# Mask pieces written during group 0's own ranked units, exponents and squares shifted to ScalarE, and small loads moved, in a four-layer graph network

## The chip, the cores and the metric

The kernel runs on one core of a Trainium2 chip. The metric is the device time of one execution in microseconds (us). The engines are TensorE (PE in the profile), VectorE (DVE), ScalarE (ACT), GpSimd (POOL) and SyncE (SP), the last of which issues most transfers. Each engine takes its instructions in the order in which the program issued them.

## The reference

A graph of 3327 nodes with 64 features passes through four layers, each of which is `x = x + f(relu(layernorm(x)), adj)` with the same dense 3327 x 3327 matrix `adj` (few entries are not zero):

```python
# layer 0: two gated cells, h -> relu(ggc(h))
m = adj @ (x @ W); gi = m @ wih.T + bih; gh = x @ whh.T + bhh   # r, z, n gates, as in a GRU
# layer 1: only the pattern of adj and each entry's rank in its row count
mask = (adj != 0); rank = cumsum(mask, axis=1); deg = rank[:, -1:]
k = minimum(deg, 100.0); pos = rank - (deg - k)
w = mask * where(pos > 0, 0.5 ** (k - pos), 0.0)
out = w @ (input @ weight) + bias
# layer 2: w = adj * adj; three times x = (w @ x) @ W.T + b
# layer 3: twice x = tanh(concat([adj @ x, x]) @ W[k])
```

So there are eight products with an N x N matrix, called hops: hops 0 and 1 use `adj` (PLAIN), hop 2 the ranked weights (RANKED), hops 3 to 5 the squares (SQUARED), hops 6 and 7 `adj` again.

## The kernel before, in words

**Tiles and units.** The nodes are padded to 2 x 13 blocks of 128. The 13 block columns are cut into four chunks (3, 3, 3 and 4 blocks, thus 384 or 512 columns for each of two halves), and the chunks into two groups, chunks 0 and 1 in group 0 and chunks 2 and 3 in group 1. A `Tile` is one of 26 source blocks of `adj`'s transpose for one group, 768 or 896 KB; 20 buffers (`slots`) hold tiles and, in halves of a buffer, masks. A unit is (hop, chunk, tile): it multiplies the tile's columns with the features of the source block into the chunk's PSUM sum (`propagate`, L561).

**Order.** `alone` and `joint` write a list of 914 units by hand. A tile serves two successive hops of its group before it is dropped, so group 0 and group 1 alternate: after group 0's hops 1 and 2, group 1 does hops 2 and 3. A unit is *own* where its source block lies in the group that it computes. The last 26 units of group 0's hop 2 (288 to 313 in the list) are own ones, two of them special; units 314 on are those of group 1's hop 2, two per tile, and its first hop-3 unit is 326.

**Looking ahead.** `run` goes through the list. In step i it issues loads up to 44 units ahead while buffers are free, makes masks up to 24 units ahead (`make_mask`, which takes room for a mask and queues two pieces), prepares squares 6 units ahead (`prepare`, L404) and expands ranked weights 3 units ahead (`expand`), and then propagates unit i.

**A ranked unit.** A mask piece is one VectorE instruction of 127 x 896 (or 768) elements (L427), and the last row comes by a small transfer from GpSimd's queue (L432). `expand` multiplies the mask by the triangular matrix `tri` on TensorE (`mm`, L271), for the two halves s = 0 and 1, and turns each half into the bits of a power of two, on ScalarE (L477) or on VectorE (L475). A tile's pieces are written by `mask_pieces(1)` once per step, except in group 0's own units, or are forced by `expand` (L468) where they are not there yet. The special unit adds the last rows of all blocks from a list, `lastw`, made by `last_sources` (L512 to L531).

**Ends of hops.** When a chunk's sum is complete, a generator (`after_0` to `after_7`) is begun. What it does is cut by `yield us`, and it continues when the scheduler's count of TensorE time (`spend`) has gone that far, or at once where something needs its result (`finish`). `after_1` ends with the layer norm and the three-term split of y[2] and, later, with `add_row(c, 3)` (L795), which adds layer 1's bias to x. `after_2` evacuates the sum (L702 or L704), does the dense product with `bd`, adds to x (L789), and makes y[3] by `layernorm_relu` (L767 to L782): sums, mean, difference, squares (on VectorE at L774 or on ScalarE at L772), their sum, a power on GpSimd (L778), and the product. The special unit of a chunk finishes the generators of the other chunks.

**Constants.** `more_constants` is such a generator, too: it loads the weights of the second cell (`load_cell(1)`), the dense weights `bd`, the last layer's `w3` (w in the profile), and the bias rows `brow`.

Of the kernel before, what the change touches and what calls it, by code (L numbers as in the profile page):

```python
# [52 lines left out]
NC = 4  # L53
PARTS = (4, 5)
CWM = 512
GROUPS = [(0, 1), (2, 3)]
# [35 lines left out]
def upper(n):  # L92
    return slice(n * D, (n + 1) * D)
# [3 lines left out]
def kernel(  # L97
# [58 lines left out]
    def unfold_cell(cell):  # L156

        n = 3 * D + (NBIAS if cell == 0 else 0)
        i, ps = take()
        for h in range(2):  # L160
            nc.tensor.matmul(ps[upper(h), :n], ident[:, :D], stage[:, 4 * D:4 * D + n], start=True, stop=True)
        v = ps[:, :3 * D].rearrange("p (g f) -> p g f", f=D)
        for h in range(2):
            nc.vector.tensor_copy(cells[upper(1 - h), cell, h, 0:3], v[upper(1 - h)])
        if cell == 0:
            nc.vector.tensor_copy(bcol, ps[:, 3 * D:n])
        give(i)
# [36 lines left out]
    def more_constants():  # L204
        nc.gpsimd.memset(stage, 0.0)
        nc.gpsimd.memset(cells, 0.0)
        for c in range(NC):
            for h in range(2):
                nc.gpsimd.memset(both[c][upper(h), h], 0.0)
        nc.gpsimd.memset(bd, 0.0)  # L210
        yield 5.0
        load_cell(0)
        yield 20.0
        unfold_cell(0)
        yield 1.0

        full = work.tile([P, P], BF16, name="t2")
        nc.gpsimd.memset(full, -TWO7)
        nc.gpsimd.affine_select(out=tri, in_=full, pattern=[[-1, P]], compare_op=ALU.is_gt, fill=0.0,
                                base=0, channel_multiplier=1)  # L220
        nc.gpsimd.affine_select(out=tri, in_=tri, pattern=[[-1, P]], compare_op=ALU.not_equal, fill=TWO7 * TWO7,
                                base=0, channel_multiplier=1)
        nc.gpsimd.memset(tri[:, P - 1:P], 0.0)
        nc.gpsimd.memset(bitsb, BITS)
        nc.gpsimd.memset(lasty, 0.0)
        wide = work.tile([P, P], F32, name="t2")
        nc.gpsimd.memset(wide, 0.0)

        for i, (bi, bh) in enumerate(((BI1, BH1), (BI2, BH2))):
            nc.vector.tensor_add(bsum[:, i], bcol[:, bi:bi + 2], bcol[:, bh:bh + 2])  # L230

        nc.vector.tensor_scalar(wide[0:D], wide[0:D], bcol[0:D, BL1:BL1 + 1], None, op0=ALU.add)
        yield 3.0
        i, ps = take()
        mm(ps[:, :D], wide, ident[:, :D])
        nc.vector.tensor_copy(brow[:, 3], ps[:, :D])
        give(i)
        yield 1.0
        yield from fold_cell(0)
        for c in range(NC):  # L240
            yield 1.0
            ahead_of_cell(c)
        yield 50.0
        load_cell(1)
        yield 10.0
        for h in range(2):
            nc.sync.dma_start(out=bd[upper(h), :, upper(h)], in_=weights[:, WL1:WL3])
            for i in range(2):
                nc.sync.dma_start(out=w3[upper(h), :, i], in_=weights[:, WL3 + (h + i) % 2:NW:2])
        yield 10.0  # L250
        unfold_cell(1)
        yield from fold_cell(1)
        yield 20.0
        nc.sync.dma_start(
            out=brow[:, 0:3],
            in_=bass.AP(tensor=bias_rows.tensor, offset=bias_rows.offset, ap=[[0, P], [D, 3], [1, D]]),
        )
# [35 lines left out]
    def give(i):  # L293
        released[i] = max(released) + 1
        (idle_sums if i < 4 else idle_temps).append(i)
# [29 lines left out]
    def begin(c, task):  # L325
        finish(c)
        tasks[c] = [task, 0.0]
        advance(c)
# [5 lines left out]
    def later_task(us, task):  # L334
        yield us
        yield from task
# [10 lines left out]
    y = [[None] * NC for _ in range(8)]  # L347
# [90 lines left out]
    def mask_pieces(n=0, t=None):  # L438

        while pieces and (n > 0 or any(u is t for u, _, _ in pieces)):  # L440
            _, half, piece = pieces.popleft()
            piece(half)
            n -= 1

    def expand(k, c, t):

        if k == COUNT:
            return None
        w = width(c)
        if t is SPECIAL:  # L450
            g = c // 2
            w0 = (CH[c][0] - CH[GROUPS[g][0]][0]) * P
            finish(NC + 1 + g)
            return lastw[g][:, w0:w0 + w].bitcast(BF16)
        if KIND[k] == PLAIN or (KIND[k] == SQUARED and t.in_place):
            return t.view(c)
        if KIND[k] == SQUARED:
            room = Mask(t.w)
            wide = room.view.rearrange("p s w -> p (s w)").bitcast(F32)[:, :2 * w].rearrange("p (s w) -> p s w", s=2)
            square(wide, t.view(c), t.q + c)  # L460
            squared[k, c, t] = room
            return wide
        wide = work.tile([P, 2, CWM], I16, name="e", bufs=4)[:, :, :w]

        mask_pieces(t=t)  # L468
        for s in range(2):
            i, ps = take()  # L470
            mm(ps[:, :w], tri, t.mask.view[:, s, t.cols(c)])
            own = chunk_of(t.q % NB) in GROUPS[t.g]
            busy = any((k - 1, ch) in sums for ch in GROUPS[t.g])
            if s and (own if t.g == 0 and (own or busy) else c == GROUPS[t.g][1] or t.g == 1 and not own):
                nc.vector.tensor_scalar(wide[:, s], ps[:, :w], BITS, 0.0, op0=ALU.add, op1=ALU.max)  # L475
            else:
                nc.scalar.activation(wide[:, s], ps[:, :w], AF.Relu, bias=bitsb)  # L477
            give(i)
        spend(STREAM_US * w / CWM * 0.5)
        if c == GROUPS[t.g][1]:  # L480
            t.mask.free()
        return wide.bitcast(BF16)
# [182 lines left out]
    def run():  # L665
        total = {}
        for k, c, t in units:
            total[k, c] = total.get((k, c), 0) + 1
        done = {}
        loaded, masked, prepared, expanded = 0, 0, 0, deque()  # L670
        for i, (k, c, t) in enumerate(units):
            while loaded < len(units) and loaded < i + LOAD:
                u = units[loaded][2]
                if u is not SPECIAL and u.slot is None:
                    if len(dead) <= RESERVE and loaded > i + EXPAND:
                        break
                    u.load()
                loaded += 1
            while masked < min(loaded, i + MASK):
                if is_masked(*units[masked]):  # L680
                    if not spare and len(dead) <= RESERVE + 1:
                        break
                    make_mask(units[masked][2], RANKED)
                masked += 1
            while prepared < min(loaded, i + PREPARE):
                prepare(*units[prepared])
                prepared += 1
            while len(expanded) < min(EXPAND + 1, len(units) - i):
                assert prepared > i + len(expanded)
                expanded.append(expand(*units[i + len(expanded)]))  # L690
            if k != 2:
                mask_pieces(1 + len(pieces) // 6)
            elif not (c in GROUPS[0] and (t is SPECIAL or chunk_of(t.q % NB) in GROUPS[0])):
                mask_pieces(1)
            n = done[k, c] = done.get((k, c), 0) + 1
            propagate(k, c, t, expanded.popleft(), n == 1, n == total[k, c])

# [183 lines left out]
    def after_1(c, acc):  # L881
        pace = 1.0 if c in GROUPS[0] else 1.2
        at, h2T = yield from gru(acc, c, BI2, BH2, 1, pace)
        v = transpose_to_nodes(h2T, c)
        dead.append(at)
        yield 0.8 * pace
        residual(v, c, relu=True)
        yk = nodes(c)
        yield from layernorm_relu(yk, c, TWO27, 1.2 * pace, squares_on_scalar=c in GROUPS[1])
        y[2][c] = yield from in_three(yk, c)  # L890
        yield 45.0 if c in GROUPS[1] else 25.0
        add_row(c, 3)

    def after_2(c, acc):
        m = evacuate(acc, c)
        yield 1.4
        v = dense_to_nodes(m, WL1, c)
        yield 1.2
        residual(v, c)
        yk = nodes(c)  # L900
        yield from layernorm_relu(yk, c, pace=1.0)
        y[3][c] = yk
        yield 15.0
        add_row(c, 2)
# [67 lines left out]
            begin(c, before_0(c))  # L972
    begin(NC, more_constants())
    begin(NC + 1, later_task(70.0, last_sources(0)))
    begin(NC + 2, later_task(175.0, last_sources(1)))
    run()
    for c in list(tasks):
        finish(c)
# [39 lines left out]
```

## Time and profile before

| | us |
|---|---|
| median of 3 runs | 721.21 |
| lowest, highest of them | 721.14, 725.19 |
| profiled execution | 720.42 |
| its span, first to last instruction | 718.2 |
| TensorE busy in the span | 685.5 (95%) |
| VectorE busy | 343.5 (48%) |
| ScalarE busy | 264.4 (37%) |
| GpSimd busy | 79.2 (11%) |

A line of the profile names an engine, a source line, an operation, the tile written and the tile read, the size, and the number of instructions. In a timeline the first two numbers are start and duration in us, and a bracket at the end tells how long the engine had been idle and what ended it. In the page's slices each digit is a fortieth of the span.

### The profile page before, as it was taken

The page shows a single profiled execution, that of the slowest core. Times are in us where ns is not written, and L with a number is a line of the kernel's source. Part 1 is how long each engine was busy: PE and PEld are TensorE (multiplying, and loading weights), DVE is VectorE, ACT ScalarE, POOL GpSimd, SP SyncE. Part 2 cuts the span into 40 slices and gives each one's busy share as a digit, 9 for nine tenths or more (in the row PEclk, how much of TensorE's full clock was granted, in tenths as well). Part 3 has the DMA queues.
Part 4 walks back from the last instruction along what each step waited for, and adds up shares of the span by engine and source line. Part 5 has one row for each costly group of instructions (what it writes and reads, how often), then busy time and mean ns, then how long its engine had stood idle before and what let it go on. Part 6 is the DMA issues. An engine that isn't in the chain of part 4 may idle for free.

```text
span 718.2 us, 12625 instructions
## 1 busy us (share of the span) xinstructions
PE 685.5 (95%) x5128; PEld 354.0 (49%) x5128; DVE 343.5 (48%) x700; ACT 264.4 (37%) x403; POOL 79.2 (11%) x114
## 2 busy tenths in 40 slices
PE   1999999999999986999999999999999999999997
PEld 1454667544556763546444444334444444344464
DVE  7467736635987878847615102421162466005101
ACT  1014000302147853789999322850065700000101
POOL 4300000001491303212100000000010000000000
PEclk9999999999999998999999999999999999999999
DMA  9999994299678651492799839971997399927991
GB/s 346 401 386 405 406 395 160 61 374 377 228 272 315 232 191 52 144 320 92 243 359 373 285 109 406 405 295 57 375 372 260 116 391 405 405 97 262 400 402 39
DMA packets 68549, 201.31 MB, mean 280 GB/s; under 512 B 7228, under 2 KB 8228, under 8 KB 68492
## 3 DMA queue, kind: packets, MB, share of 16 engines
q1 hardware_dynamic: 65596, 199.46, 74.9%
q8 instruction: 40, 0.66, 0.4%
q10 hardware_dynamic: 720, 0.85, 0.3%
q0 software_dynamic: 2176, 0.20, 0.2%
q14 instruction: 17, 0.14, 0.1%
HBM read 199.45 MB, written 0.85 MB: 279 GB/s over the span
## 4 chain that ended last, share of the span: by engine, by line
PE 54%; ACT 4%; issue 1%; DVE 0%; ACTq 0%
PE sum L561 50%; ACT adj L404 4%; PE temp L271 3%; PE temp L723 1%; DVE both L758 0%; ACT both L757 0%; ACT t L702 0%; DVE xs L951 0%; PE sum L271 0%; ACTq L953 0%; ACT t L948 0%; ACTq L404 0%; ACT e L477 0%; ACTq L757 0%; ACTq L948 0%
## 5 line engine op out<-in xcount | busy, mean ns | idle before, releaser
L561 PE MATMUL sum<-adj,y 128*64 128x384 f32 (+3 forms) x3016 | 531.1, 501 | 2.1 <-DVE e L475 0.9
L561 PEld LDWEIGHTS sum<-adj,y 128*64 128x64 f32 x3016 | 228.6, 137 | 248.9 <-issue 222.7
L404 ACT ACTIVATE adj<-adj 128x768 f32<-128x768 f32 (+1 forms) x174 | 142.6, 890 | 49.5 <-PE sum L561 23.7
L427 DVE TENSOR_SCALAR adj<-adj 128x768 bf16<-128x768 f32 (+3 forms) x208 | 113.1, 594 | 37.8 <-PE temp L496 33.9
L477 ACT ACTIVATE e<-temp,bitsb 128x384 int16<-128x384 f32 (+1 forms) x114 | 64.7, 607 | 28.7 <-PE temp L271 19.7
L561 PE MATMUL sum<-e,both 128*64 128x384 bf16 (+1 forms) x624 | 74.6, 347 | 0.0
L758 DVE COPY both<-sum 64x384 f32<-64x384 f32 (+3 forms) x17 | 9.7, 568 | 115.6 <-ACT both L757 114.5
L757 ACT COPY both<-sum 64x384 f32<-64x384 f32 (+3 forms) x17 | 8.1, 478 | 153.0 <-PE sum L561 147.4
L406 DVE TENSOR_TENSOR adj<-adj 128x768 f32<-128x768 f32 (+1 forms) x34 | 32.6, 1010 | 53.5 <-DMA adj<-in_adjT 33.6
L778 POOL TENSOR_TENSOR st<-st,mhalf 128x6 f32<-128x6 f32 (+1 forms) x16 | 23.8, 1486 | 303.9 <-DVE st L776 303.9
L271 PE MATMUL temp<-adj,tri 128*64 128x384 bf16 (+1 forms) x334 | 51.7, 347 | 5.9 <-DVE adj L427 5.7
L561 PEld LDWEIGHTS <-both 128*64 128x64 bf16 x624 | 40.8, 112 | 19.3 <-issue 6.6
L432 POOL DMA_DIRECT2D adj<-totals x52 | 31.4, 605 | 119.9 <-DVE adj L836 74.8
L475 DVE TENSOR_SCALAR e<-temp 128x384 int16<-128x384 f32 (+1 forms) x53 | 32.2, 609 | 22.4 <-PE temp L271 10.7
L271 PEld LDWEIGHTS <-tri 128*64 128x64 bf16 x416 | 28.5, 112 | 27.7 <-issue 16.0
L752 DVE STREAM_TRANSPOSE both<-y 32x96 f32<-32x96 f32 (+1 forms) x128 | 35.6, 278 | 2.9
L704 DVE COPY t<-sum 128x384 f32<-128x384 f32 x8 | 4.4, 556 | 60.9 <-PE sum L561 60.9
L496 PE MATMUL temp<-adj,behind 128*64 128x384 bf16 x208 | 30.2, 339 | 0.9 <-DVE adj L427 0.7
L496 PEld LDWEIGHTS <-behind 128*64 128x64 bf16 x208 | 16.8, 110 | 17.7 <-issue 16.5
L702 ACT COPY t<-sum 128x384 f32<-128x384 f32 (+1 forms) x8 | 4.2, 529 | 54.2 <-PE sum L561 54.2
L914 DVE TENSOR_TENSOR y<-temp,brow 128x384 f32<-128x384 f32 (+1 forms) x8 | 4.7, 592 | 29.6 <-PE temp L271 29.6
L271 PE MATMUL sum<-adj,tri 128*64 128x384 bf16 (+1 forms) x82 | 15.5, 342 | 3.2 <-DVE adj L427 3.1
(121 smaller groups left out, 321.2 us busy)
## 6 DMA issues: line engine op xcount, KB each, us to landing
adj<-in_adjT SPq DMA_DIRECT2D x130, 768.0 KB, 8.8
adj<-in_adjT SPq DMA_DIRECT2D x104, 896.0 KB, 11.9
xs<-in_x SPq DMA_DIRECT2D x1, 640.0 KB
adj<-totals POOLq DMA_DIRECT2D x26, 3.0 KB, 4.8
adj<-totals POOLq DMA_DIRECT2D x26, 3.5 KB, 2.0
out<-xs ACTq DMA_DIRECT2D x2, 192.0 KB
out<-xs ACTq DMA_DIRECT2D x1, 256.0 KB
stage<-in_weights SPq DMA_DIRECT2D x2, 112.0 KB, 14.2
```

The source lines that it names most:

```text
L271: nc.tensor.matmul(out[hs], lhsT[:, hs], rhs, start=start, stop=stop)
L404: nc.scalar.activation(sq, v, AF.Square)
L406: nc.vector.tensor_tensor(sq, v, v, ALU.mult)
L427: nc.vector.tensor_scalar(t.mask.view[:rows, half], t.view()[:rows, half], 0.0, None, op0=ALU.not_equal)
L432: nc.gpsimd.dma_start(out=t.mask.view[P - 1:P], in_=totals[t.g][t.q:t.q + D + 1:D, :])
L475: nc.vector.tensor_scalar(wide[:, s], ps[:, :w], BITS, 0.0, op0=ALU.add, op1=ALU.max)
L477: nc.scalar.activation(wide[:, s], ps[:, :w], AF.Relu, bias=bitsb)
L496: nc.tensor.matmul(counts[c][1][s * D:(s + 1) * D, :w], behind[:, NQ - 1 - t.q:NQ - 1 - t.q + D], t.mask.view[:, s, t.cols(c)], start=firs ...
L561: nc.tensor.matmul(acc[h][1][h * D:(h + 1) * D, :w], yq[h], rhs[h], start=first and n == 0, stop=last and n == len(terms) - 1)
L752: nc.vector.transpose(to[at:at + 32, :, q], h[q * 32:(q + 1) * 32, :, s, f * 32:(f + 1) * 32])
L758: nc.vector.tensor_copy(both[c][upper(1), 1], acc[1][1][upper(1), :width(c)])
L778: nc.gpsimd.tensor_tensor(st[:, 3, :n], st[:, 2, :n], mhalf[:, :n], ALU.pow)
```

## The change

- In `run`, group 0's own units of hop 2 now call `mask_pieces(1)` too, in each third step, once y[2] of chunks 0 and 1 is there.
- In `expand`, while y[3] of chunk 0 or 1 is not there, a unit of group 1 with a source of group 0 gives the half s = 1 to VectorE only for chunk 3; chunk 2 gives both to ScalarE. Before, both chunks gave it to VectorE.
- In `after_2`, the squares of the layer norm of chunks 0 and 1 are taken by ScalarE.
- In `after_1`, the bias of layer 1 is added after 14 us of the scheduler's count for chunks 0 and 1 (25 before) and after 80 for chunks 2 and 3 (45 before).
- In `more_constants`, the second cell's weights are unfolded before `bd` and `w3` are loaded; those loads and that of `brow` come later by 41 and 15 us of the scheduler's count.
- `last_sources(1)` begins at 140 us of that count instead of 175.

```diff
@@ more_constants
         load_cell(1)
-        yield 10.0
+        yield 20.0
+        unfold_cell(1)
+        yield from fold_cell(1)
+        yield 30.0
         for h in range(2):
             nc.sync.dma_start(out=bd[upper(h), :, upper(h)], in_=weights[:, WL1:WL3])
             for i in range(2):
                 nc.sync.dma_start(out=w3[upper(h), :, i], in_=weights[:, WL3 + (h + i) % 2:NW:2])
-        yield 10.0
-        unfold_cell(1)
-        yield from fold_cell(1)
-        yield 20.0
+        yield 5.0
         nc.sync.dma_start(
             out=brow[:, 0:3],
...
@@ expand
             busy = any((k - 1, ch) in sums for ch in GROUPS[t.g])
-            if s and (own if t.g == 0 and (own or busy) else c == GROUPS[t.g][1] or t.g == 1 and not own):
+            if t.g == 1 and not own and any(y[3][ch] is None for ch in GROUPS[0]):
+
+                on_vector = s and c == GROUPS[1][1]
+            else:
+                on_vector = s and (own if t.g == 0 and (own or busy) else c == GROUPS[t.g][1] or t.g == 1 and not own)
+            if on_vector:
                 nc.vector.tensor_scalar(wide[:, s], ps[:, :w], BITS, 0.0, op0=ALU.add, op1=ALU.max)
             else:
                 nc.scalar.activation(wide[:, s], ps[:, :w], AF.Relu, bias=bitsb)
@@ run
             elif not (c in GROUPS[0] and (t is SPECIAL or chunk_of(t.q % NB) in GROUPS[0])):
                 mask_pieces(1)
+            elif i % 3 == 0 and all(y[2][ch] is not None for ch in GROUPS[0]):
+                mask_pieces(1)
@@ after_1
-        yield 45.0 if c in GROUPS[1] else 25.0
+        yield 80.0 if c in GROUPS[1] else 14.0
         add_row(c, 3)
@@ after_2
-        yield from layernorm_relu(yk, c, pace=1.0)
+        yield from layernorm_relu(yk, c, squares_on_scalar=c in GROUPS[0])
@@ tile_adj_gnn_stack_kernel
-    begin(NC + 2, later_task(175.0, last_sources(1)))
+    begin(NC + 2, later_task(140.0, last_sources(1)))
```

## The prediction, made before the changed kernel was run

> **What bounds the kernel now.** I read the page's slices first, then what TensorE waited for, then the busy table for the one stage that stands out, then that stage instruction by instruction.
>
> ```profile
> span 718.2 us, 12625 instructions
> PE   1999999999999986999999999999999999999997
> PEclk9999999999999998999999999999999999999999
> ```
> TensorE is the bound almost everywhere; its idle time is 718.2 - 685.5 = 32.7 us. Of it 15.0 is the start and some 4 the last 10 us. The only hole in between is in slices 15 and 16 (about 263 to 293 us), where the granted clock drops too.
>
> ```profile
> PE temp L740 <- DVE y L782: 15.0, 1, 15.0
> PE temp L271 <- DVE adj L427: 5.7, 6, 1.7
> PE sum L271 <- DVE adj L427: 3.1, 3, 2.1
> PE sum L561 <- DVE e L475: 0.9, 1, 0.9
> PE sum L561 <- DMA adj<-in_adjT: 0.7, 1, 0.7
> ```
> TensorE's waits: us in total, times, longest. After the start, what it waits for is VectorE: the ranked product by `tri` (L271) waits for the mask pieces of L427 (5.7 + 3.1 us).
>
> ```profile
> core 0: us, PE busy (x) PEld busy (x) DVE busy (x) ACT busy (x) POOL busy (x), PEclk, DMA share, GB/s
> 246.60:264.10 17.50, 17.41 (x218) 14.76 (x213) 14.46 (x28) 11.95 (x21) 1.01 (x2) 1.00 0.60 194
> 264.10:293.60 29.50, 19.82 (x166) 11.32 (x163) 24.48 (x49) 12.96 (x20) 10.03 (x13) 0.88 0.22 76
> 293.60:340.00 46.40, 46.40 (x414) 25.28 (x416) 30.86 (x55) 39.86 (x65) 7.03 (x13) 1.00 0.63 215
> 340.00:376.00 36.00, 35.17 (x264) 16.51 (x262) 14.55 (x27) 34.61 (x45) 2.98 (x2) 1.00 0.83 288
> ```
> The row 264 to 294: TensorE 19.82 of 29.5, VectorE 24.48, ScalarE only 12.96, transfers 0.22. VectorE paces this stage. In the row before (group 0's own ranked units) VectorE still has 3.0 us free, and no mask piece is written there.
>
> ```profile
> 263.77 0.54 DVE L789 TENSOR_TENSOR xs<-xs,temp 128x384 f32<-128x384 f32 x1
> 264.35 0.55 DVE L767 TENSOR_REDUCE st<-xs 128x6 f32<-128x384 f32 x1
> 264.94 0.17 DVE L768 TENSOR_SCALAR st<-st 128x6 f32<-128x6 f32 x1
> 265.15 0.56 DVE L769 TENSOR_TENSOR t<-xs,st 128x384 f32<-128x384 f32 x1
> 265.62 1.16 DVE L427 TENSOR_SCALAR adj<-adj 127x896 bf16<-127x896 f32 x2
> ...
> 269.67 0.55 DVE L774 TENSOR_TENSOR y<-t 128x384 f32<-128x384 f32 x1
> 270.26 0.55 DVE L775 TENSOR_REDUCE st<-y 128x6 f32<-128x384 f32 x1
> 270.84 0.17 DVE L776 TENSOR_SCALAR st<-st 128x6 f32<-128x6 f32 x1
> 270.92 1.16 DVE L427 TENSOR_SCALAR adj<-adj 127x896 bf16<-127x896 f32 x2
> ```
> VectorE in time order. The masks of group 1's first tiles are forced by `expand` (L468), three units before use, and stand in VectorE's queue behind the layer norm of group 0's chunk 0. TensorE idles 2.12 us to 266.29 and 1.68 us to 271.60 on these two pairs.
>
> **The Trainium skill.** "TensorE: Matmul & The Clock Gate", Part 1, says that the array falls to half clock after about a window of 3.4 us with little activity and returns after a busy one; the trace agrees (0.85 and 0.83 in 260-270 and 280-290, each behind over 2 us of idling, 1.00 elsewhere). "Perfetto Trace Analysis", Identifying the Most-Contended Engine, calls matmul busy time a bad measure; so here: the stage's busy 19.8 us covers only 14.3 us of work (below). "VectorE: DVE Perf Modes", Why PSUM operands drop a tier, explains why a piece of 896 elements from SBUF costs little more than an exponent instruction of 384 from PSUM; the trace: 0.54-0.62 us and 0.47-0.55.
>
> **Prices**, start to start in the trace. TensorE: `tri` products 0.33 (384 wide) and 0.43 (512), ranked sums 0.49 and 0.65, dense 0.66. VectorE: exponents (L475) 0.47 and 0.60, mask piece 0.54, L789, L767, L774, L775 0.58 each, L769, L782, L795, L704 0.47 each, L768 and L776 0.2. ScalarE: exponents 0.47 and 0.60, a square of 384 0.52 (L772). GpSimd's power 1.35 to 1.6.
>
> **What the stage could be.** From the first tri product of group 1 (266.29) to the start of the first squared unit (291.89) TensorE has 7 x (0.33 + 0.43) = 5.3 of tri products, 3 x 0.49 + 6 x (0.49 + 0.65) = 8.3 of sums and 0.66 dense: 14.3 us. Counted from 264.17, where TensorE ran dry, it took 27.7. So 13.4 us is the most that can be won before 292, and another 0.9 at 293.59.
>
> **The change, part by part.**
>
> *Mask pieces in own units.* The 26 own units last from about 246.6 to 272 now. Pieces can be queued from the fourth on (the horizon is 24 units); one in three units writes one: 8 pieces, the first four tiles. Both chunks' y[2] is complete when they begin (last L854 at 243.67). The tiles were issued for loading from 209 to 218, so no load is waited for. Cost: 0.54 per three units, 0.18 a unit; with the exponents 0.65 of TensorE's 0.81 per unit. It fits: 4.3 us for all eight against the 3.0 us that VectorE had free in that row and the 1.5 us of the list of last rows (L524 and L528, 0.5 + 1.0 at 250-252), which moves 35 us earlier by the scheduler's count, to about 216, where VectorE's row of mask pieces has just ended and TensorE is busy with plain units; ScalarE's 1.0 us (L530) goes with it. If this cover were missing, each piece would cost TensorE its 0.54. On GpSimd the pieces' row copies (L432, 0.54 each) now go out ahead of norm 0's power instead of behind it. What remains open is a wait for the mask's room, last read by recent tri products: 0 to 0.8 us a piece; I take 0, as the exponents before it wait for later tri products.
>
> *Exponents to ScalarE.* While group 0's y[3] is missing, the chunk-2 half goes to ScalarE: 0.47 less for each of the six or seven tiles to 291, with ScalarE 44% busy there. VectorE per tile: 2 x 0.54 + 0.60 = 1.7 instead of 2.15, TensorE 1.9.
>
> *Squares to ScalarE.* L774 goes from both norms: 2 x 0.58 less, with one wait of VectorE for ScalarE each, 0 to 1 us; I take 0 to 0.3. *Bias rows* (L795): chunks 0 and 1 go to about 256, and chunks 2 and 3 are forced at the special unit of chunk 0 instead: 0.47 + 0.60 there against 2 x 0.47 now. Nothing won.
>
> *Small weights.* Six DMAs (`bd`, `w3`; about 0.62 us of SP each, 3.7 in all, at 124-128) and `brow` (170) move to roughly 175-185 on SP, between loads that wait for room anyway; `bd` is read first at 262. Cover: the loads stand 44 units ahead. At best the 0.65 us wait for a load at 129.35 goes; 0 to 0.65 either way, I take 0.4 won.
>
> **The new stage, worked along the queues.** With the masks there, tri products never wait; the sums wait for exponents behind the norms.
> - Special unit of chunk 0 (260): a piece, two bias rows and L704 end at 262.45, 0.65 later than now, so TensorE is at the first group-1 tri product at 264.65.
> - Norm 0: L789 to L769 end at 266.7; an exponent 0.6, a piece, L775, L776 to 268.6. The special unit of chunk 1 then finishes this norm at once: L782 waits for GpSimd's power, to 270.3, with VectorE idle 1.7; L782 and L795 to 271.3, the next exponent to 271.9. TensorE waits 1.0.
> - Norm 1: 1.9 us of VectorE at 274-276, ahead of exponents: TensorE waits 1.5, then (L775, L776, two pieces) 0.9, then 0.7.
> Sum: 264.65 + 14.3 + 4.1 = 283.1 for the first squared unit, against 291.89: 8.8 us. The next unit starts at 283.75 against 293.59, since VectorE has made up its arrears: 9.8. No idle stretch reaches 2 us, so the half clock should go (its price is inside the 13.4). With the load wait 10.2.
>
> Profiled execution: 720.42 (span 718.2 and 2.2 around it) - 10.2 = 710.2; the median of the runs shown is 0.8 above it, so **711.0**.
>
> **Rivals.**
> - *VectorE still paces* (0.18). Its work did not shrink much: two norms (2 x 3.4 us) and two power waits (2 x 1.6) come to 10 us, and each can stall TensorE almost in full because exponents stand behind them in one queue. For: VectorE's 24.5 of 29.5. Against: three units of lookahead (2.5 us). Then some 9 of the 13.4 us stay: gain 4.5, 716.5.
> - *ScalarE gives it back* (0.07). It takes 7 x 0.47 + 2 x 0.52 = 4.3 us more, and is 34.6 of 36 us busy at 340-376, where the chain of waits runs through L404. If it reached that stage late, the 4.3 us would be paid there: 715.3. Against: it gains 0.45 us a tile on TensorE after 294.
> - *Slower* (0.04): each of the 8 pieces in own units holds VectorE until the room's last reader is done; VectorE cannot run ahead, and each costs the round trip of a tri product and exponent (0.33 + 0.56 + 0.25) with its own 0.54: 1.7 each, 13.5 in all, against 10.2 won: 724.5. It decides from 10.2/8 = 1.3 us a piece on.
>
> **Numbers.** The forecast's case (706 to 713.9) has 0.71: its stalls of 4.1 us could be 0.5 or 7. A measurement tells about 1% (7.2 us) from no change. Faster by over 1% (below 714.0) 0.71; within 1% 0.25 (the first two rivals); slower by over 1% 0.04. Range 706 to 717: most of the stalls gone, to VectorE still pacing.
>
> **What would show it.** Right: eight L427 pieces between 246 and 264, no wait of L271 for L427, clock 1.00 throughout, six or seven chunk-2 exponents on ScalarE, squares L772 twice more, VectorE idle 1 to 2 us ahead of L782 near 270, TensorE waits for L475 of 3 to 5 us in all, and the first squared unit near 283. Wrong: TensorE gaps between 248 and 262 (the slower case), over 7 us of waits for L475 (first rival), or a distance to before that shrinks after 340 (second).

## The result and the profile after

The changed kernel takes 712.87 us (median of 4 runs, 711.7 to 713.05) against 721.57 of the kernel before: 8.7 us less. The ratio is 0.9869, with a 95% interval from 0.9839 to 0.9899. The forecast was 711.0 us in a range from 706 to 717. The profiled execution took 712.98 us, with a span of 710.9.

The page's head and slices:

```profile
span 710.9 us, 12617 instructions
PE   1999999999999998999999999999999999999997
PEclk9999999999999999999999999999999999999999
```

The hole of slices 15 and 16 is down to a single 8, and the drops of the granted clock are gone. What TensorE waited for (us in total, times, longest), without the 14.9 us at the start:

```profile
PE sum L271 <- DVE e L480: 2.1, 2, 1.1
PE sum L566 <- DVE e L480: 1.8, 2, 1.6
PE sum L566 <- DMA adj<-in_adjT: 0.9, 2, 0.7
```

(Lines move by 5 to 7 in the changed file: the exponents on VectorE are L480 for L475, the sums L566 for L561, the power L785, and the product behind it L789.) No tri product waits for a mask any more. What is left in the stage are waits for exponents and one of 0.76 us for the evacuation of chunk 0's sum. The table by stage, engines from left to right as before:

```profile
246.60:264.10 17.50, 16.82 (x208) 14.27 (x203) 15.63 (x32) 11.89 (x21) 4.03 (x7) 1.00 0.41 124
264.10:284.00 19.90, 17.31 (x188) 12.82 (x190) 17.57 (x36) 14.47 (x27) 7.71 (x10) 1.00 0.38 127
```

The second row ends before the second hop-3 unit (286.29), where TensorE waits once more. Counted between the same units, from 4.5 us after the special unit of chunk 0 to the second hop-3 unit, the stage that took 29.5 us takes 20.7. VectorE is still the busiest engine in the row, 17.57 of 19.9 us against TensorE's 17.31.

**Where the 8.7 us are.** I cut each trace at three points: the special unit of chunk 0, the first hop-3 unit, and the ranked unit that follows the second hop-3 unit. From here on "the stage" is the time from the first of these points to the third.

| trace | special unit | first hop-3 unit | ranked unit after two | special to ranked | ranked to end |
|---|---|---|---|---|---|
| before | 259.61 | 291.89 | 294.50 | 34.89 | 423.75 |
| changed | 261.11 | 283.83 | 287.20 | 26.09 | 423.75 |

The stage gives 8.80 us, and what follows it takes the same 423.75 us in both. The spans differ by 7.3 only, because the changed kernel's profiled execution comes to the stage 1.5 us later. Most of that, 1.1 us, is at the start, where the program is the same; the first 48 sums:

```profile
16.34 8.70 PE L561 MATMUL sum<-adj,y 128*64 128x384 f32 x48
```

```profile
16.26 9.82 PE L566 MATMUL sum<-adj,y 128*64 128x384 f32 x48
```

The first line is of the kernel before, the second of the changed one. Over the traces of this study, from the first sum to the first counting product (L496, or L501 in the changed file), which follows these sums, it is 8.4 to 9.9 us, whatever the kernel: the records have TensorE at full clock from 17.9 us in the kernel before and from 20.1 in the changed one. A single profile is thus uncertain by about 1 us before the stage begins, and the experiments below are read by their stage as well as by their time.

**The share of the clock.** Up to the first hop-3 unit the stage is 9.6 us shorter. TensorE's busy time for the same products fell there from 23.4 to 19.4 us, and its idle time from 8.9 to 3.3 (the rows stand under "More pieces" below). The kernel before has two stretches of 3.4 us at half clock (granted clock 0.5) in it, the changed kernel none. So some 4 of the 9.6 us are busy time, most of it the clock, and 5.6 are waits that are gone.

### The profile page after: what moved, and what is told of

Same layout as the page of the kernel before. It is cut to its first block, busy times and chain, and to the rows that moved or that the text cites. A ratio compares the mean times of both kernels' runs of the same rounds, so it can differ in the third digit from the quotient of the medians.

```text
span 710.9 us, 12617 instructions
## 1 busy us (share of the span) xinstructions
PE 682.9 (96%) x5128; PEld 353.9 (50%) x5128; DVE 338.7 (48%) x692; ACT 267.4 (38%) x411; POOL 79.5 (11%) x114
## 4 chain that ended last, share of the span: by engine, by line
PE 57%; DVE 3%; DMA 1%; ACT 1%; issue 0%; POOL 0%; ACTq 0%; DVEq 0%; POOLq 0%; SPq 0%
PE sum L566 53%; PE temp L271 3%; PE temp L730 1%; DMA adj<-in_adjT 1%; DVE e L480 1%; DVE adj L427 1%; POOL st L785 0%; DVE both L765 0%; ACT both L764 0%; DVE st L774 0%; ACT e L482 0%; DVE xs L796 0%; PE sum L271 0%; DVE st L782 0%; ACT adj L404 0%
## 5 line engine op out<-in xcount | busy, mean ns | idle before, releaser
L566 PE MATMUL sum<-adj,y 128*64 128x384 f32 (+3 forms) x3016 | 532.4, 502 | 3.1 <-DVE e L480 1.6
L566 PEld LDWEIGHTS sum<-adj,y 128*64 128x64 f32 x3016 | 228.8, 137 | 251.0 <-issue 222.3
L427 DVE TENSOR_SCALAR adj<-adj 128x768 bf16<-128x768 f32 (+3 forms) x208 | 113.3, 593 | 39.0 <-PE temp L501 35.0
L566 PE MATMUL sum<-e,both 128*64 128x384 bf16 (+1 forms) x624 | 73.1, 339 | 0.4 <-DVE e L480 0.2
L482 ACT ACTIVATE e<-temp,bitsb 128x384 int16<-128x384 f32 (+1 forms) x117 | 66.2, 607 | 18.6 <-PE temp L271 13.5
L785 POOL TENSOR_TENSOR st<-st,mhalf 128x6 f32<-128x6 f32 (+1 forms) x16 | 24.3, 1516 | 291.1 <-DVE st L783 291.1
L432 POOL DMA_DIRECT2D adj<-totals x52 | 37.0, 714 | 124.3 <-DMA adj<-in_adjT 74.8
L566 PEld LDWEIGHTS <-both 128*64 128x64 bf16 x624 | 40.6, 110 | 19.2 <-issue 6.7
L480 DVE TENSOR_SCALAR e<-temp 128x384 int16<-128x384 f32 (+1 forms) x50 | 30.5, 611 | 21.1 <-PE temp L271 9.8
L271 PEld LDWEIGHTS <-tri 128*64 128x64 bf16 x416 | 28.1, 110 | 17.9 <-issue 10.0
L501 PE MATMUL temp<-adj,behind 128*64 128x384 bf16 x208 | 30.1, 339 | 0.9 <-DVE adj L427 0.7
L501 PEld LDWEIGHTS <-behind 128*64 128x64 bf16 x208 | 16.8, 110 | 17.7 <-issue 16.5
L535 ACT ACTIVATE lastw<-adj,bitsb 128x768 int16<-128x768 f32 (+1 forms) x2 | 2.0, 990 | 44.7 <-DVE adj L533 44.7
## 6 DMA issues: line engine op xcount, KB each, us to landing
stage<-in_weights SPq DMA_DIRECT2D x2, 112.0 KB, 14.3
```

Source lines behind the costliest of these rows:

```text
L271: nc.tensor.matmul(out[hs], lhsT[:, hs], rhs, start=start, stop=stop)
L427: nc.vector.tensor_scalar(t.mask.view[:rows, half], t.view()[:rows, half], 0.0, None, op0=ALU.not_equal)
L432: nc.gpsimd.dma_start(out=t.mask.view[P - 1:P], in_=totals[t.g][t.q:t.q + D + 1:D, :])
L501: nc.tensor.matmul(counts[c][1][s * D:(s + 1) * D, :w], behind[:, NQ - 1 - t.q:NQ - 1 - t.q + D], t.mask.view[:, s, t.cols(c)], start=firs ...
L566: nc.tensor.matmul(acc[h][1][h * D:(h + 1) * D, :w], yq[h], rhs[h], start=first and n == 0, stop=last and n == len(terms) - 1)
L785: nc.gpsimd.tensor_tensor(st[:, 3, :n], st[:, 2, :n], mhalf[:, :n], ALU.pow)
```

## The experiments

Two theories were set against each other. The *queue* theory is that of the prediction: VectorE paces the stage through its one queue, and each us taken off it there is worth about one. The *latency* theory: the tri products waited for masks forced at the last moment, so the pieces alone bring nearly everything. Neither theory names the clock, and no experiment holds it fixed; where a trace shows that it moved, the text says so.

### One part alone, on the kernel before

**The mask pieces** (`e1_pieces`):

```diff
             elif not (c in GROUPS[0] and (t is SPECIAL or chunk_of(t.q % NB) in GROUPS[0])):
                 mask_pieces(1)
+            elif i % 3 == 0 and all(y[2][ch] is not None for ch in GROUPS[0]):
+                mask_pieces(1)
```

> The kernel before with only the mask pieces in group 0's own ranked units. Queue theory (mine): in the stage from 264 to 294 every us taken off VectorE's queue is worth about one us to TensorE; the eight pieces take 8 x 0.54 = 4.3 us out of it, so 4 to 5 us faster (717), and TensorE then waits for L475 behind the norms. Latency theory (rival): what cost time was that tri products had to wait for masks that were forced at the last moment; the pieces alone then bring nearly all of the 8.7 us (713 to 714), and the exponents and squares next to nothing.

Measured: 716.3 us, ratio 0.9933 [0.992, 0.9946], some 4.8 us faster. TensorE's waits for L427 in the stage are gone, and others stand in their place:

```profile
PE sum L561 <- DVE e L475: 3.4, 4, 1.8
PE sum L271 <- DVE e L475: 2.8, 3, 1.5
```

That is the queue theory's number, and the latency theory by itself is out: once the masks are there, TensorE waits 6.2 us for exponents instead. But the number does not show the queue theory's reason. Both stretches at half clock are gone too, which is 2.9 us less busy time of TensorE up to the first hop-3 unit. And in the kernel before VectorE itself waited for tri products (264 to 294 us), which it does nowhere in the stage here:

```profile
DVE e L475 <- PE sum L271: 2.2, 3, 1.3
DVE e L475 <- PE temp L271: 1.9, 4, 0.6
```

**The exponents** (`e2_exponents`), the condition `on_vector` in `expand` alone:

```diff
+            if t.g == 1 and not own and any(y[3][ch] is None for ch in GROUPS[0]):
+                on_vector = s and c == GROUPS[1][1]
...
```

> The kernel before with only chunk 2's exponents on ScalarE while y[3] of group 0 is missing. Queue theory: six or seven instructions of 0.47 off VectorE, 3 us faster (718.5). Latency theory: the tri products still wait for forced masks, within 1 us of before.

Measured: 719.31 us, ratio 0.9969 [0.9958, 0.9981], 1.7 us faster by the medians and 2.2 by the ratio. Tri products still wait for forced masks (4.1 and 3.9 us in all, 0.8 less than before), yet the kernel is faster; that speaks for the queue theory, with some 2 for 3. Its trace does not settle it. The stage is 2.35 us shorter, but only one of the two stretches at half clock is left (clock 0.94 from the special unit to the first hop-3 unit, against 0.89):

```profile
260.87:290.81 29.94, 21.87 (x217) 14.04 (x213) 23.34 (x48) 16.73 (x28) 9.16 (x12) 0.94 0.29 94
```

A stretch of 3.4 us at half clock is worth about 1.7 us (an estimate, half its length), so how much of the 2.35 is VectorE's queue stays open.

**The squares** (`e3_squares`):

```diff
-        yield from layernorm_relu(yk, c, pace=1.0)
+        yield from layernorm_relu(yk, c, squares_on_scalar=c in GROUPS[0])
```

> The kernel before with only the squares of the two norms on ScalarE. Queue theory: 2 x 0.58 off VectorE, 1 us faster (720.5) if ScalarE returns them in time. Latency theory: 0, or up to 1 us slower for the two round trips.

Measured: 720.05 us, ratio 0.9986 [0.9977, 0.9995]: 1 us faster, though the stage in its trace is only 0.46 shorter.

**The moves** (`e4_moves`): the weights, the bias rows and the last rows.

```diff
-        yield 45.0 if c in GROUPS[1] else 25.0
+        yield 80.0 if c in GROUPS[1] else 14.0
...
-    begin(NC + 2, later_task(175.0, last_sources(1)))
+    begin(NC + 2, later_task(140.0, last_sources(1)))
```

> The kernel before with only the moves: bias rows, small weights, and the list of last rows. Both theories: within 0.5 us of before. By my prediction 0.4 us faster, as the wait for a load near 129 should go; the trace of the changed kernel still has that wait (0.66 us) and a new one of 0.25 near 213, by which it should be 0 to 0.5 us slower.

Measured: 721.03 us, ratio 1.0004 [0.9996, 1.0012]. Nothing. The stage in its trace is 0.7 us shorter all the same; there, too, one of the two stretches at half clock is missing, while the waits are longer.

### One part taken out of the changed kernel

Each is the changed kernel with one hunk put back as it was.

```diff
# e5_no_pieces
-            elif i % 3 == 0 and all(y[2][ch] is not None for ch in GROUPS[0]):
-                mask_pieces(1)
# e6_no_exponents
-            if t.g == 1 and not own and any(y[3][ch] is None for ch in GROUPS[0]):
-                on_vector = s and c == GROUPS[1][1]
...
# e7_no_squares
-        yield from layernorm_relu(yk, c, squares_on_scalar=c in GROUPS[0])
+        yield from layernorm_relu(yk, c, pace=1.0)
# e8_no_moves
-        yield 80.0 if c in GROUPS[1] else 14.0
+        yield 45.0 if c in GROUPS[1] else 25.0
...
```

> The changed kernel without the mask pieces in own units. Queue theory: it loses 4 to 5 us of the gain (717). Latency theory: it loses nearly all of it (720 to 721).

> The changed kernel with chunk 2's exponents back on VectorE. Queue theory: VectorE has 3 us more to do in the stage, 3 us of the gain go (716). Latency theory: within 1 us of the changed kernel.

> The changed kernel with the squares of the two norms back on VectorE. Queue theory: 1 us slower than the changed kernel (714). Latency theory: the same, or up to 1 us faster, as the two round trips to ScalarE go.

> The changed kernel without the moves of bias rows, small weights and last rows. By the prediction 0.4 us slower than the changed kernel (713.3); by the trace, which shows a new wait of 0.25 near 213, 0.2 to 0.5 us faster, unless the list of last rows at 250 gets in the way of the eight pieces, which would make it up to 1.5 us slower.

| kernel | median | less than before, by the medians | ratio to before | stage, us | stage against changed |
|---|---|---|---|---|---|
| changed | 712.87 | 8.7 | 0.9869 [0.9839, 0.9899] | 26.09 | |
| without pieces | 718.23 | 2.4 | 0.9965 [0.9953, 0.9977] | 33.40 | +7.3 |
| without exponents | 714.29 | 6.3 | 0.991 [0.9893, 0.9927] | 28.42 | +2.3 |
| without squares | 712.91 | 7.7 | 0.9884 [0.9866, 0.9904] | 27.30 | +1.2 |
| without moves | 712.09 | 8.5 | 0.9878 [0.9861, 0.9895] | 26.07 | 0.0 |

The changed kernel was measured beside a kernel before of 721.57 us, the other four beside one of 720.62, so the gains over the kernel before compare better than the medians. The pieces are worth more as the last part (6.3 us by the medians, 7.3 by the stage) than as the first (4.8 and 5.3). What is lost lies between the two theories' forecasts for this run. Without the pieces the tri products wait for masks again, and 6.8 us at half clock are back (clock 0.89 up to the first hop-3 unit):

```profile
PE sum L271 <- DVE adj L427: 3.8, 4, 2.1
PE temp L271 <- DVE adj L427: 3.5, 5, 1.9
```

The exponents are worth 2.4 by the medians and 2.3 by the stage as the last part, with no stretch at half clock in either trace; that is the queue theory's best case, with 2.3 for 3. The squares are worth 1.0 and 1.2. By the times alone only the pieces are told from the spread, since the intervals of the other rows overlap with that of the changed kernel. The moves are worth nothing in either place, and the list of last rows at 250 does not disturb the eight pieces.

### What is left of the waits

Three edits of the changed kernel, each aimed at one wait that its trace shows.

**The bank** (`e9_bank`). TensorE waits 1.62 us before the second hop-3 unit, for an exponent on VectorE, though hop 3 reads no exponents. The changed kernel's TensorE and VectorE there:

```profile
283.83 0.84 PE L566 MATMUL sum<-adj,y 128*64 128x384 f32 x4
286.29 1.08 PE L566 MATMUL sum<-adj,y 128*64 128x512 f32 x4 [1.62 <-DVE e L480]
```

```profile
285.55 0.68 DVE L480 TENSOR_SCALAR e<-sum 128x512 int16<-128x512 f32 x1
```

Followed through `take`, the sum of chunk 3 opens in the very bank that `expand` of unit 329 had used one step earlier; that exponent reads a `sum` bank (e<-sum).

```diff
         for s in range(2):
-            i, ps = take()
+            early_sums = t.g == 1 and all(y[3][ch] is not None for ch in GROUPS[0]) and not any((3, ch) in sums for ch in GROUPS[1])
+            i, ps = take(either=not early_sums)
```

> The changed kernel, where tri products that are expanded between the end of group 0's norms and the first hop-3 unit take only temp banks. In the changed kernel TensorE waits 1.62 us at 286.29 for an exponent of VectorE, though a hop-3 unit reads none: by my theory its sum opens in the PSUM bank that the last exponent (of unit 329) had only just left. Then this wait goes and the kernel is 1 to 1.6 us faster than the changed one (711.3 to 712). Rival: the wait is for the tile's square, or for VectorE's arrears as such; then the wait stays or moves to the next unit and the time is within 0.5 us of 712.9.

Measured: 710.52 us, ratio 0.985 [0.9833, 0.9867], 10.5 us below the kernel before of the same runs, where the changed kernel was 8.7 below its own; the stage is 24.22 us, 1.9 shorter. All other waits of the stage are the same to 0.01 us. The wait is gone, both hop-3 units run on (x8), and the exponent of unit 329 on VectorE, now read from a `temp` bank, comes at 285.30 without anyone waiting:

```profile
283.58 1.70 PE L567 MATMUL sum<-adj,y 128*64 128x384 f32 x8
285.08 0.68 PE L567 MATMUL sum<-e,both 128*64 128x384 bf16 x6
```

```profile
285.30 0.68 DVE L481 TENSOR_SCALAR e<-temp 128x512 int16<-128x512 f32 x1
```

So the wait was for the bank, and neither for the tile's square nor for VectorE's arrears as such.

**The power** (`e10_fill`). In the changed kernel VectorE idles while GpSimd takes the power of chunk 0's norm:

```profile
269.46 0.54 DVE L782 TENSOR_REDUCE st<-y 128x6 f32<-128x384 f32 x1
...
271.75 0.56 DVE L789 SCALAR_TENSOR_TENSOR y<-t,st 128x384 f32<-128x384 f32 x1 [1.54 <-POOL st L785]
```

```diff
         nc.gpsimd.tensor_tensor(st[:, 3, :n], st[:, 2, :n], mhalf[:, :n], ALU.pow)
+        mask_pieces(fill)
         yield 1.5 * pace
...
+        yield from layernorm_relu(yk, c, squares_on_scalar=c in GROUPS[0], fill=2 if c == 0 else 0)
```

> The changed kernel with two mask pieces put between GpSimd's power and the product that waits for it, in the norm of chunk 0. There VectorE idles 1.54 us in the changed kernel. Queue theory: 2 x 0.54 of work fall into that idle time, 1 us faster (711.9). Rival: the same two pieces delay the product and with it the exponent behind it, nothing won, within 0.3 us of 712.9.

Measured: 712.75 us, ratio 0.9882 [0.9866, 0.9899]: nothing, as the rival had it. The idle time does shrink, yet counted from the special unit the product (L790 here, L789 in the changed kernel) starts 0.24 us later, at 10.88 in place of 10.64, and the tri product behind it waits 1.29 us in place of 1.06:

```profile
271.47 0.56 DVE L790 SCALAR_TENSOR_TENSOR y<-t,st 128x384 f32<-128x384 f32 x1 [0.70 <-POOL st L785]
```

The two pieces do not hold the product up in VectorE's queue, where 0.70 us stay idle behind them. It is the power that takes longer, first in the changed kernel, then here:

```profile
270.37 1.35 POOL L785 TENSOR_TENSOR st<-st,mhalf 128x6 f32<-128x6 f32 x1 [16.04 <-DVE st L783]
```

```profile
269.85 1.58 POOL L785 TENSOR_TENSOR st<-st,mhalf 128x6 f32<-128x6 f32 x1 [16.04 <-DVE st L783]
```

**More pieces** (`e11_half`):

```diff
-            elif i % 3 == 0 and all(y[2][ch] is not None for ch in GROUPS[0]):
+            elif i % 2 == 0 and all(y[2][ch] is not None for ch in GROUPS[0]):
```

> The changed kernel with a mask piece in each second own unit in place of each third: eleven pieces instead of eight. VectorE is busy 15.6 of 17.5 us in that stretch. Queue theory: 3 x 0.54 more leave the stage behind it, 1 to 1.6 us faster (711.3 to 712). Rival (the slower case of the prediction, in small): own units are now full, the pieces push the exponents and the evacuation of chunk 0, and what is won behind is lost there: within 0.5 us of 712.9 or up to 1 us slower.

Measured: 712.61 us, ratio 0.9888 [0.9866, 0.991]: nothing. In part the rival is right: the evacuation of chunk 0 comes later, TensorE waits 1.07 us for it in place of 0.76, and the stage is 0.3 us longer. Why the earlier pieces win nothing behind it is seen from the special unit to the first hop-3 unit:

```profile
259.60:291.90 32.30, 23.39 (x217) 14.67 (x213) 26.51 (x54) 13.59 (x22) 9.39 (x12) 0.89 0.27 87
```

```profile
260.10:286.00 25.90, 20.54 (x217) 14.11 (x214) 23.97 (x51) 13.76 (x22) 7.85 (x10) 1.00 0.33 109
```

```profile
261.10:283.80 22.70, 19.42 (x216) 14.34 (x212) 20.24 (x42) 16.01 (x30) 7.51 (x10) 1.00 0.39 124
```

```profile
262.10:285.20 23.10, 19.51 (x218) 14.43 (x215) 21.29 (x44) 16.07 (x30) 6.24 (x8) 1.00 0.37 121
```

These are the kernel before, the pieces alone, the changed kernel and the one with more pieces. VectorE's busy and idle time in this stretch is 26.5 + 5.8, then 24.0 + 1.9, then 20.2 + 2.5, then 21.3 + 1.8 us. Mask pieces (L427) that VectorE starts in it: 16, 13, 13 and 14; with the two pieces under the power 15. As long as pieces are queued, every step behind the own units writes one whether it is urgent or not. A piece written earlier therefore need not leave the stretch; it makes room for the next one. The changed kernel writes five pieces ahead of the special unit and has three fewer behind it; the one with more pieces writes seven ahead and has two fewer.

**All three** (`e12_all`), the three diffs above together:

> The three edits together (temp banks, two pieces under the power, pieces in each second own unit). Queue theory: the stage has some 4.9 us of waits left; the three take 3 to 4 us of them, 709 to 710. If the waits are what bank and lookahead impose, it gains no more than the best of the three alone.

Measured: 710.11 us, ratio 0.9852 [0.9834, 0.987], which is not to be told from the bank alone (stage 24.76 us against 24.22). The 0.54 us more are the two waits just seen, 1.07 for 0.76 and 1.29 for 1.06. The bank edit is what counts; with it the kernel is 1.5% faster than before.

## Why the prediction was right, and where it was off

- *The place.* Right: the whole gain lies between the special unit of chunk 0 and the second hop-3 unit, and the 423.75 us behind it are the same in both. ScalarE gave nothing back at 340-376, so that rival is out. The first rival (VectorE still paces) had some 9 us stay; 4.9 us of waits are left up to the second hop-3 unit, 4.0 of them for exponents on VectorE.
- *Pieces in own units cost nothing.* Right for all but one. They are written from 250.01 on, between the exponents, and TensorE has no gap before the dense product; the slower rival had nothing to stand on. The piece just ahead of chunk 0's evacuation does cost its 0.54: the dense product waits 0.76 us (the second fence) and 0.22 where the pieces are taken out (e5). Six of the eight pieces, not all, are begun by 264; the last two, also issued in own units, come at 265.95 and 268.93.

```profile
250.01 0.62 DVE L427 TENSOR_SCALAR adj<-adj 127x896 bf16<-127x896 f32 x1
```

```profile
264.18 0.88 PE L271 MATMUL temp<-bd,t 128*64 128x128 f32 x12 [0.76 <-DVE t L711]
```

- *Steps of the new stage.* By the sum the first tri product of group 1 comes 5.04 us after the special unit, and it does (266.15). Norm 0: VectorE idle 1.7 ahead of L789, measured 1.54; TensorE 1.0, measured 1.06 (at 273.44). It was the next tri product that waited, not the sum: two sums and six banks make three units of lookahead, and the tri product needs the bank that the late exponent still holds.
- *Norm 1 was overrated.* The sum had 1.5 + 0.9 + 0.7 = 3.1 us; TensorE waited 1.05 + 0.23 + 0.18 = 1.5. On the other side the products, waits taken off, took 15.2 us where the prices add up to 14.3. That the sum comes out near for the first hop-3 unit is thus in part luck: two errors of opposite sign.
- *"VectorE has made up its arrears"* is the step that failed. The prediction let the second hop-3 unit follow at once; it waited 1.62 us for its bank, which the sum had put at nothing. Up to the first hop-3 unit the stage gained 9.6 us (32.28 to 22.72) where 8.8 was forecast; with the second it is 8.8 where 9.8 was forecast.
- *The value of a piece.* The forecast had the pieces' 4.3 us leave VectorE's stage. The counts show 3 fewer, 16 to 13, which is 1.6 us. With the pieces alone VectorE's busy time fell by 2.5 us and its idle time by 3.9: since no tri product waits for a mask, VectorE no longer waits for tri products. Size right, reason half right.
- *The small weights.* No gain of 0.4 us. In the changed kernel's trace the wait for a load stays, and there is a new one:

```profile
130.41 0.87 PE L566 MATMUL sum<-adj,y 128*64 128x384 f32 x4 [0.66 <-DMA adj<-in_adjT]
212.89 1.51 PE L566 MATMUL sum<-adj,y 128*64 128x384 f32 x8 [0.25 <-DMA adj<-in_adjT]
```

The load behind the first wait lands 5.7 us after its issue with the six small transfers right behind it (before) and without them (changed), so they did not make it late. A single trace says little here: over all traces the first wait is 0.38 to 0.91 us in the five kernels without the moves, and in the nine with them from none shown to 0.66; the second stands in four of these nine only (0.25 to 1.68) and in none of the five. What of this is the weights' new place (188 to 193 on SP), and what the last rows taken earlier, was not separated.
- *The clock.* Right that the half clock goes: 1.00 in the whole stage against 0.89 before. But the prediction's reading that the trace agrees with "TensorE: Matmul & The Clock Gate", Part 1, holds only in part. The page has the clock fall after an idle window of about 3.4 us, and calls the window free-running. But in the kernel before a wait of 2.12 us was enough, and then one of 1.53 with one of 0.78; the measurement decides. Nor does an idle stretch of 2 us decide by itself, as the last section shows. (Two small slips: between 270 and 280 the clock is 0.97, not 1.00, since the first of the two stretches ends at 270.5; and the 19.8 us of busy time beside the 14.3 of work are of 264.1 to 293.6, where 266.29 to 291.89 has 18.9.)

Of the 1.9 us between forecast and median, 1.0 is in the stage and 0.4 is the gain that the weights did not bring; the rest is within the spread of the runs.

## What to carry to other kernels

When an in-order engine paces a stage, write down its busy and its idle time there: moving work off it lowers the first, and breaking a wait that goes round two engines (mask to product to exponent) lowers the second; of what the pieces alone won up to the first hop-3 unit, VectorE's busy time gave 2.5 us (1.6 of them the three pieces fewer) and its idle time 3.9. Look at the granted clock as well, before a gain is put down to either: of the same 6.4 us, 2.9 were busy time of TensorE. Work done ahead pays only if something later is skipped: a helper with a fixed rate per step fills the place again; a rate that falls with the lead would be the next thing to try, and it was not tried here. And where a product waits for an engine whose result it does not read, look at which buffer it writes.

## What the runs showed of the hardware that I had not expected

- The stretch from the first sum to the first counting product, the same instructions in every kernel, takes 8.4 to 9.9 us, with the moment at which the full clock is granted (between about 18 and 21 us after the start in these traces). In a comparison of two profiles that is as much as a small edit is worth.
- In all 14 traces every later change of the clock lies a multiple of 3.41 us after that moment. What counted in the stage was how long TensorE idled within one window of this grid: behind the seven windows with 2.0 to 2.3 us of idling the clock was halved for 3.41 us (once for 6.83), behind those with 1.8 or less it was not. A wait of 2.11 us that fell across two windows left the clock alone (e2). The two rows are a window of the kernel before, with the half clock behind it, and the window of e2 with most of that wait, without:

```profile
263.69:267.10 3.41, 1.11 (x13) 0.57 (x10) 2.98 (x7) 0.37 (x2) 0.00 (x0) 1.00 1.01 370
```

```profile
265.95:269.36 3.41, 1.62 (x17) 1.11 (x18) 2.02 (x5) 1.17 (x3) 0.00 (x0) 1.00 0.85 305
```

- The time of GpSimd's power on 128 x 6 elements went with what VectorE was doing. In the norms of chunks 0 and 1 in the 14 traces it takes 1.35 us in the 12 cases in which no mask piece is running when it begins, and 1.58 to 2.08 in the 16 in which one is. Why was not tested.
- One PSUM bank opened just after an exponent had read it cost 1.6 us of waiting in the trace; when other banks were used, the stage was 1.9 us shorter.
